# The first block's conditional layer: block-diagonal weights against two half tiles in TensorE's rows

## The chip, the cores and the metric

The kernel runs on one core of a Trainium2 chip. The core has five engines that run side by side and meet at semaphores: TensorE (PE in the profile; its weight loads are shown as PEld), VectorE (DVE), ScalarE (ACT), GpSimd (POOL) and SyncE (SP), which here only issues DMAs. The metric is the device time of one execution in microseconds; less is better. The program has 43659 instructions on the chip, and most of them belong to parts that the change leaves alone.

## The reference

The input x has 64 sequences of 64 rows (c) and 1024 columns (t). The layer that the change touches is the very first one:

```python
W = weights[condition]                     # 16 matrices of 64x64, one chosen per sequence
return jnp.einsum('bct,bcd->bdt', x, W)    # y[b, d, t] = sum over c of x[b, c, t] * W[b, c, d]
```

The full computation is an attention block on y with a residual, and then a second conditional layer (a routed low-rank addition to a dense product) with a quantized feed-forward block and a second residual:

```python
x = x + attn(cond(x, itok_B_0_15, weights), qkvw, qkvb, ow, ob)
x = x + ffn(cond2(x, itok_B_0_7, W, Wr, A, B), ...)
```

In the attention, each row d of y is a token with 1024 features t, so the products with qkvw contract over t. Everything is f32 here.

## The kernel before, in words

**Tiles and blocks.** Two sequences stacked give a tile of 128 rows (2 x 64) by 1024 columns; there are 32 tiles. Four tiles are a block (512 tokens), and there are eight blocks. The attention stage goes block by block, and within a block over four groups of heads: products for q and k, for v, then scores, softmax and context of the group before are woven in between.

**The seven-product scheme.** Products with qkvw aren't done directly. Tokens and features are split into quarters, and seven products on quarters and on sums of quarters take the place of eight (class Winograd, with the order of products in `ORDER` and their operands in `A_OF` and `B_OF`). On the side of the tokens the quarters are B11, B12, B21 and B22: the first digit is the half of the features (t below or above 512), the second the half of the block's tokens (tiles 0 and 1, or 2 and 3). The sums are T1 = B12 - B11, T2 = B22 - T1, T3 = B22 - B12 and T4 = B21 - T2, made by `t_of` (L358) on VectorE, T4 in B12's place. On the side of the weights they are S1 to S4, made by `sums` (L276, four lines L282, L283, L284 and L279) from the raw quarters A11, A21, A22 and A12.

**Product order of the first q job.** The first job (q, head group 0) takes its products in the order 1, 2, 6, 7, 5, 4, 3: A11 by B11 into bank a, A12 by B21 into the same bank, S2 by T2 into bank b, S3 by T3 into c, S1 by T1 into d, A22 by T4 into c, S4 by B22 into d. Each of these is eight records of TensorE at L509 (four f32 products, two records each). The names in the profile are psqa to psqd; the k job behind it has pska to pskd, the v job psva to psvd. Before product 2 is written into bank a, ScalarE copies the bank away (psqp, L479).

**The conditional layer of blocks 1 to 7.** `conditional_tile` (L400) lets the gathered 64x64 matrix stand in TensorE and passes x, one matrix in each half of the rows. Its result has d in the rows and t in the columns, and it is transposed by DMA. That takes long, and the work of other blocks hides it.

**The conditional layer of block 0.** There is nothing to hide it behind, so `conditional` (L367) makes a result that is transposed already: x stands, and the weights pass. `load_x` (L246) loads tile j, and POOL issues an indirect DMA (L253) that gathers the two 64x64 matrices of its two sequences into wg, 128 rows by 64 columns. VectorE fills a tile wbd with zeros (L345), and copies each wg into the two diagonal blocks of its 128x128 part (L395, two copies a tile). So one product with 128 contracted rows serves both sequences: 128 columns of x stand, the 128 columns of wbd pass, and the result has t in its rows and the tile's 128 tokens in its columns. Four such products (L380) fill one PSUM bank, which is one tile (j) and one half of t (hf). VectorE copies even tiles into the B quarter (L386), ScalarE odd ones (L388).

The order is written out by hand: the four tiles with the lower half of t, then tiles 2, 3, 0, 1 with the upper half. That way B11 and B12 are ready first, T1 is computed after the fourth product group, T2 and T3 after the sixth, and T4 after the last.

**What sets the order.** `run` (L693) takes a triple (cost, product, rest): it issues the product on TensorE, then the rest (copies and sums) of the triple before it, which waits in `behind`. The cost only advances the planner's clock `now`, from which later pieces of softmax and context get their due times. Each engine executes its own instructions strictly in the written order. PSUM tiles named "g" come from a pool of four banks, so a fifth bank waits until the first one has been copied away.

**Behind the conditional layer**, the weights' sums are issued as one list, `first_sums` (L771): four for wq on VectorE and the store of wq's S parts by a POOL DMA (L300), four for wk on POOL and their store, four for wv on POOL. POOL executes them in this order, so its store of wq, which waits for VectorE's last sum, stands ahead of the sums of wk and wv. SP's next load of a q weight goes into the buffer of the first one: it waits for that store and for the last product of the first q job.

Of the kernel before, what the change touches and what calls it, by code (L numbers as in the profile page):

```python
# [11 lines left out]
F32 = mybir.dt.float32  # L12
# [8 lines left out]
P = 128  # L21
# [15 lines left out]
def adaln_attn_ffn(ctx: ExitStack, tc: tile.TileContext, a, out: bass.AP):  # L37
# [40 lines left out]
    with tc.manual_schedule(), ExitStack() as psum, ExitStack() as early:  # L78
        ps_g = psum.enter_context(tc.tile_pool(name="ps_g", bufs=4, space=PSUM, reuse_waits="tile"))
        st = early.enter_context(tc.tile_pool(name="halve", bufs=2))  # L80
        chores = halve_weights(tc, st, const, dram, srcs, half, any_i)
        chores = itertools.chain(chores, combine_quarters(tc, st, (("wo", a["ow"]), ("wt", a["w_t"])), comb))
        op = OutProjection(tc, a, x_t, out_t, ctx_d, x1_d, ps_g, comb, KC, H)
        attention(tc, a, x_t, ctx_d, ident, dram, ps_g, KC, PB, NBLK, NCH, HPC, H, C, chores, early, op)
        second_stage(tc, a, out_t, x1_d, ident, ps_g, KC, NT, H, C, half, comb, op)
# [99 lines left out]
def attention(tc, a, x_t, ctx_d, ident, dram, ps_g, KC, PB, NBLK, NCH, HPC, H, C, chores, early, op):  # L185
# [6 lines left out]
    nc = tc.nc  # L192
    BLK = PB * P
    HB = BLK // 2
    KQ = KC // 2
# [6 lines left out]
    halves = [slice(r * C, (r + 1) * C) for r in range(2)]  # L202
# [16 lines left out]
    with ExitStack() as ctx, ExitStack() as mid:  # L219
        def pool(stack, name, bufs, **kw):  # L220
            return stack.enter_context(tc.tile_pool(name=name, bufs=bufs, reuse_waits="tile", **kw))
# [8 lines left out]
        yp = pool(mid, "y1", 1, side="right")  # L230
# [30 lines left out]
        x_of = {}  # L261
# [29 lines left out]
        def load_qk(b, wh, c, eng=None):  # L291
            t = w_qk[b, wh, c] = wp.tile([P, 7, KQ, P], F32, tag="wqk", name=f"w{wh}_{b}_{c}")
            if b == 0:
                if (wh, c) == ("q", 0):
                    held(t[:, SLOT["A11"], 0, 0:1], x_of[0, 0][1])
                for key in RAW:
                    nc.sync.dma_start(t[:, SLOT[key], :, :], quarter(key, (0 if wh == "q" else H) + c * P, P))
                return sums(
                    eng or nc.vector, lambda key: t[:, SLOT[key], :, :],
                    lambda: nc.gpsimd.dma_start(qk_d[wh, c], t[:, NR:7, :, :]),  # L300
                )
            for key in RAW:
                if SLOT[key] < NR:
                    nc.sync.dma_start(t[:, SLOT[key], :, :], quarter(key, (0 if wh == "q" else H) + c * P, P))
            nc.sync.dma_start(t[:, NR:7, :, :], qk_d[wh, c])
# [31 lines left out]
        first_sums = load_qk(0, "q", 0) + load_qk(0, "k", 0, nc.gpsimd)  # L337
# [3 lines left out]

        wbd = yp.tile([P, KC, P], F32, tag="B21", name="wbd")
        nc.vector.memset(wbd, 0.0)  # L345
        vals = [
            act.tile([P, PB, 2, 4, 2, HD], F32, tag=f"vals{g}", name=f"vals{g}") for g in range(NV)
        ]
# [2 lines left out]
        B = {}  # L351

        def quarter_of(b, key):
            return (yp if b % 2 else w).tile(
                [P, KQ, HB], F32, tag=key if b % 2 else key + "e", name=f"y{key}_{b}"
            )

        def t_of(b, Y, key, x, y):  # L358
            if key == "T4":
                Y[key] = Y["B12"]  # L360
            else:
                Y[key] = yp.tile([P, KQ, HB], F32, tag=key, name=f"{key}_{b}")
            nc.vector.tensor_tensor(Y[key], Y[x], Y[y], ALU.subtract)

        T_OF = (("T1", "B12", "B11"), ("T2", "B22", "T1"), ("T3", "B22", "B12"), ("T4", "B21", "T2"))

        def conditional():  # L367

            def one(hf, j):
                key = f"B{hf + 1}{j // 2 + 1}"  # L370
                box = []

                def product():
                    xt = x_of[0, j][0]
                    if j % 2 == 0:
                        B[key] = quarter_of(0, key)
                    ps = ps_g.tile([P, 4, P], F32, tag="g", name=f"cond_{j}_{hf}")
                    for q in range(KQ):
                        k = hf * KQ + q
                        nc.tensor.matmul(ps[:, q, :], xt[:, k * P:(k + 1) * P], wbd[:, j, :], start=True, stop=True)  # L380
                    box.append(ps)

                def rest():
                    dst = B[key][:, :, (j % 2) * P:(j % 2 + 1) * P]
                    if j % 2 == 0:
                        nc.vector.tensor_copy(dst, box[0])  # L386
                    else:
                        nc.scalar.copy(dst, box[0])  # L388
                    for n in {(0, 3): (0,), (1, 3): (1, 2), (1, 1): (3,)}.get((hf, j), ()):
                        t_of(0, B, *T_OF[n])  # L390
                return 0.95, product, rest

            for j in range(PB):
                for r in range(2):
                    nc.vector.tensor_copy(wbd[halves[r], j, halves[r]], x_of[0, j][1][halves[r], :])  # L395
            return [one(0, j) for j in range(PB)] + [one(1, j) for j in (2, 3, 0, 1)]

        Ys = [{} for _ in range(NBLK)]

# [245 lines left out]
        behind = []  # L645
# [47 lines left out]
        def run(cost, product=None, rest=None):  # L693
            nonlocal now
            while due and due[0][0] <= now + 0.01:
                heapq.heappop(due)[2]()
            if product:
                product()
            if behind:
                behind.pop()()  # L700
            if later:
                later.pop(0)()
            if rest:
                behind.append(rest)
            now += cost
# [62 lines left out]

        for f in conditional():
            run(*f)  # L770
        for f in first_sums:  # L771
            f()
        for f in qk_fill(0, 0) + v_fill(0, 0):
            run(*f)
        for b in range(NBLK):
# [3 lines left out]
            for c in range(NP):  # L779
# [15 lines left out]
                elif b + 1 < NBLK:  # L795
# [4 lines left out]
                    B = Ys[b + 1]  # L800
# [1357 lines left out]
```

## Time and profile before

| | us |
|---|---|
| median of three runs | 2379.62 (2379.28 to 2385.07) |
| the profiled execution's own time | 2369.88 |
| its span, first to last instruction | 2368.0 |
| TensorE busy in the span | 2335.0 |
| products of block 0's conditional layer (L380), first start to last end | 9.74 to 19.19 |
| first product of the q job (psqa) | 19.02 |

A group's line reads: line, engine, operation, output<-inputs, shapes, and the count behind the x; then the busy time in us, the mean of one in ns, and the idle time of the engine just before them, with what ended it. A line of the timeline or of the chain reads: start in us from the span's first instruction, length in us, engine, line, operation, tiles, count. The length runs to the end of the last one of the group. The ends of products on TensorE are modelled, and they overlap the start of the next, so the pace of a row of products is the distance of their starts.

### The profile page before, as it was taken

The page shows a single profiled execution, that of the slowest core. Times are in us where ns is not written, and L with a number is a line of the kernel's source. Part 1 is how long each engine was busy: PE and PEld are TensorE (multiplying, and loading weights), DVE is VectorE, ACT ScalarE, POOL GpSimd, SP SyncE. Part 2 cuts the span into 40 slices and gives each one's busy share as a digit, 9 for nine tenths or more (in the row PEclk, how much of TensorE's full clock was granted, in tenths as well). Part 3 has the DMA queues.
Part 4 walks back from the last instruction along what each step waited for, and adds up shares of the span by engine and source line. Part 5 has one row for each costly group of instructions (what it writes and reads, how often), then busy time and mean ns, then how long its engine had stood idle before and what let it go on. Part 6 is the DMA issues. An engine that isn't in the chain of part 4 may idle for free.

```text
span 2368.0 us, 43659 instructions
## 1 busy us (share of the span) xinstructions
PE 2335.0 (99%) x17608; PEld 1721.7 (73%) x17608; DVE 1502.4 (63%) x2887; ACT 969.4 (41%) x1333; POOL 533.9 (23%) x647
## 2 busy tenths in 40 slices
PE   8999999999999999999999999999999999999997
PEld 7888888888888888888888548888645445454553
DVE  3574474474453544643634688998577878777787
ACT  1344344344353453443433522334344454444443
POOL 4121112111122223220000357887300000000001
PEclk9999999999999999999999999999999999999999
DMA  7899799899899999997976845657944444545453
GB/s 225 201 259 243 213 215 234 227 240 214 214 243 251 231 253 251 224 229 191 184 194 187 252 164 179 218 168 238 319 80 78 83 78 83 88 75 91 75 109 86
DMA packets 612116, 437.17 MB, mean 185 GB/s; under 512 B 362433, under 2 KB 524226, under 8 KB 609986
## 3 DMA queue, kind: packets, MB, share of 16 engines
q1 hardware_dynamic: 581234, 377.13, 63.7%
q0 software_dynamic: 12240, 40.38, 7.9%
q10 hardware_dynamic: 18432, 16.79, 3.0%
q8 instruction: 141, 2.31, 0.4%
q14 instruction: 69, 0.57, 0.1%
HBM read 257.24 MB, written 91.23 MB: 147 GB/s over the span
## 4 chain that ended last, share of the span: by engine, by line
PE 94%; DMA 2%; DVE 2%; ACT 1%; issue 0%; SPq 0%; POOL 0%; ACTq 0%; DVEq 0%; POOLq 0%
PE pga L1410 6%; PE psvc L530 5%; PE psva L530 5%; PE psvd L530 5%; PE psqa L509 4%; PE pskd L509 4%; PE pskc L509 4%; PE psqd L509 4%; PE psqc L509 4%; PE pbd L1129 4%; PE pska L509 4%; PE pbc L1129 4%; PE pba L1129 4%; PE pgb L1410 3%; PE psqb L509 2%; PE pr L1711 2%
## 5 line engine op out<-in xcount | busy, mean ns | idle before, releaser
L582 ACT ACTIVATE prob<-prob 128x512 f32<-128x512 f32 x128 | 80.6, 629 | 351.0 <-DVE prob L578 351.0
L442 POOL COPY yB<-yhT 128x512 int16<-128x512 int16 (+1 forms) x84 | 76.7, 969 | 436.5 <-DMA yhT<-yh 398.5
L608 ACT COPY pT<-phT 128x1024 int16<-128x1024 int16 x128 | 165.5, 1340 | 20.5 <-DMA phT<-ph 16.0
L1949 POOL DMA_DIRECT2D out_dram<-y x29 | 25.2, 868 | 651.5 <-DVE y L1941 651.5
L596 ACT COPY ph<-prob 128x1024 int16<-128x1024 int16 x128 | 133.6, 1044 | 60.7 <-DVE prob L590 40.0
L577 DVE TENSOR_REDUCE mx<-s 128x8 f32<-128x512 f32 x128 | 87.4, 683 | 68.4 <-PE s L568 68.4
L509 PE MATMUL psqa<-yB,wq 128*128 128x256 f32 x512 | 121.1, 379 | 0.5 <-ACT psqp L479 0.5
L509 PE MATMUL pska<-yB,wk 128*128 128x256 f32 x512 | 121.0, 379 | 0.0
L530 PE MATMUL psva<-wv,yB 128*128 128x256 f32 x512 | 115.8, 379 | 0.0
L1420 ACT COPY ng<-pga 128x256 f32<-128x256 f32 x125 | 46.4, 372 | 155.8 <-PE pga L1410 138.9
L1129 PE MATMUL pba<-wtA,x1T 128*128 128x512 f32 x240 | 107.9, 592 | 0.0
L1410 PE MATMUL pga<-woS,ug_T 128*128 128x256 f32 x432 | 107.4, 380 | 0.4 <-ACT ng L1420 0.3
L530 PEld LDWEIGHTS psva<-wv,yB 128*128 128x128 f32 x512 | 97.2, 190 | 14.0 <-issue 0.8
L509 PEld LDWEIGHTS psqa<-yB,wq 128*128 128x128 f32 x512 | 97.1, 190 | 14.0 <-ACT psqp L479 0.9
L509 PEld LDWEIGHTS pska<-yB,wk 128*128 128x128 f32 x512 | 97.3, 190 | 13.2
L633 ACT ACTIVATE co<-banks,bqkv 128x256 f32<-128x256 f32 x128 | 60.7, 474 | 111.7 <-PE banks L411 81.7
L590 DVE TENSOR_TENSOR prob<-prob,den 128x512 f32<-128x512 f32 x128 | 89.2, 697 | 4.4
L578 DVE TENSOR_TENSOR prob<-s,mx 128x512 f32<-128x512 f32 x128 | 88.5, 691 | 4.5
L1410 PEld LDWEIGHTS pga<-woS,ug_T 128*128 128x128 f32 x432 | 81.8, 190 | 12.4 <-issue 0.7
L544 DVE TENSOR_TENSOR vals<-psvd,psvu 64x256 f32<-64x256 f32 (+1 forms) x96 | 40.6, 422 | 76.6 <-PE psvd L530 75.7
L588 DVE TENSOR_REDUCE den<-prob 128x8 f32<-128x512 f32 x128 | 86.4, 675 | 0.0
L1576 ACT COPY x1T<-x1h 128x1024 int16<-128x1024 int16 x64 | 81.3, 1333 | 2.7 <-DMA x1h<-x_d 2.7
(318 smaller groups left out, 5394.6 us busy)
## 6 DMA issues: line engine op xcount, KB each, us to landing
wv<-v_d SPq DMA_DIRECT2D x56, 512.0 KB, 7.7
wq<-q_d SPq DMA_DIRECT2D x28, 1024.0 KB, 8.5
wk<-k_d SPq DMA_DIRECT2D x28, 1024.0 KB, 8.7
wq<-in_qkvw_dram SPq DMA_DIRECT2D x100, 256.0 KB, 3.7
wk<-in_qkvw_dram SPq DMA_DIRECT2D x100, 256.0 KB, 5.0
wv<-in_qkvw_dram SPq DMA_DIRECT2D x50, 512.0 KB, 7.1
x<-in_x_dram SPq DMA_DIRECT2D x32, 512.0 KB, 7.4
ctx_d<-co ACTq DMA_DIRECT2D x128, 128.0 KB, 7.1
```

The costliest lines, as they stand in the source:

```text
L509: nc.tensor.matmul(ps[:, 0:HB], A[:, SLOT[A_OF[i]], k, :], B[B_OF[i]][:, k, :], start=first and k == 0, stop=k == KQ - 1, skip_group_check ...
L530: nc.tensor.matmul(ps[:, j * VC:(j + 1) * VC], B[B_OF[i]][:, k, j * P:(j + 1) * P], A[:, k, :], start=first and j == 0 and k == 0, stop=k ...
L577: nc.vector.tensor_reduce(mx, ps[:, :, n, :, :], AX.X, ALU.max)
L578: nc.vector.tensor_tensor(p.rearrange("p j h k -> p h j k"), ps[:, :, n, :, :], mx.unsqueeze(3).to_broadcast([P, HPC, 2, C]), ALU.subtract,)
L582: nc.scalar.activation(p, p, AF.Exp, scale=scale)
L588: nc.vector.tensor_reduce(den, p, AX.X, ALU.add)
L590: nc.vector.tensor_tensor(p, p, den.unsqueeze(2).to_broadcast([P, n, C]), ALU.mult)
L596: nc.scalar.copy(h, planes(p.rearrange("p n k -> p (n k)")))
L608: nc.scalar.copy(planes(pT.rearrange("p a b q -> p (a b q)")), hT)
L1129: self.nc.tensor.matmul(ps, self.B[self.B_OF[i]][:, k, :], self.A[self.A_OF[i]][:, k, :], start=first and k == 0, stop=k == self.KQ - 1, s ...
L1410: nc.tensor.matmul(s[bank], B[:, k, :], A[:, k, :], start=first and k == 0, stop=k == 1, skip_group_check=True)
L1576: nc.scalar.copy(planes(x.rearrange("p k q -> p (k q)")), s.pop(("hT", n)))
```

## The change

wbd, its memset and its copies are gone. A product now contracts 64 rows: the 64 rows of x of one sequence (halves[r]) by 128 columns stand, and that sequence's gathered 64x64 matrix passes. The two sequences of a tile use the upper and the lower half of TensorE's rows, in turn, and write to two PSUM banks: box[0] and box[1], each 128 rows (t) by 8 groups (k) of 64 tokens. A tile thus has 16 products in place of 8, and each moves 64 columns in place of 128.

The layer is worked through tile by tile, both halves of t together (cost 1.3 a tile in place of 0.95 for each of eight groups). The copies are eight on VectorE (the first sequence, L390) and eight on ScalarE (the second, L392), each of 128 by 4 by 64. The token sums T1 to T4 (now L361) have moved behind the whole layer, and they are woven with VectorE's weight sums: T1, T2, S1, S2, T3, S3, T4, S4. The rest of the last tile is issued at once, ahead of them. Lines below the change are two lower than before in part of the file and two higher at its end. The orders of instructions on POOL and SP are the same as before, and so are those on the other engines behind the first q job's start.

```diff
--- before.py
+++ after.py
@@ -341,8 +341,6 @@
 
 
 
-        wbd = yp.tile([P, KC, P], F32, tag="B21", name="wbd")
-        nc.vector.memset(wbd, 0.0)
         vals = [
             act.tile([P, PB, 2, 4, 2, HD], F32, tag=f"vals{g}", name=f"vals{g}") for g in range(NV)
         ]
@@ -366,34 +364,34 @@
 
         def conditional():
 
-            def one(hf, j):
-                key = f"B{hf + 1}{j // 2 + 1}"
+            def one(j):
                 box = []
 
                 def product():
-                    xt = x_of[0, j][0]
-                    if j % 2 == 0:
-                        B[key] = quarter_of(0, key)
-                    ps = ps_g.tile([P, 4, P], F32, tag="g", name=f"cond_{j}_{hf}")
-                    for q in range(KQ):
-                        k = hf * KQ + q
-                        nc.tensor.matmul(ps[:, q, :], xt[:, k * P:(k + 1) * P], wbd[:, j, :], start=True, stop=True)
-                    box.append(ps)
+                    xt, wg = x_of[0, j]
+                    for hf in range(2):
+                        if j % 2 == 0:
+                            B[f"B{hf + 1}{j // 2 + 1}"] = quarter_of(0, f"B{hf + 1}{j // 2 + 1}")
+                    box.extend(ps_g.tile([P, KC, C], F32, tag="g", name=f"cond_{j}_{r}") for r in range(2))
+                    for k in range(KC):
+                        for r in range(2):
+                            nc.tensor.matmul(
+                                box[r][:, k, :], xt[halves[r], k * P:(k + 1) * P], wg[halves[r], :],
+                                start=True, stop=True,
+                            )
 
                 def rest():
-                    dst = B[key][:, :, (j % 2) * P:(j % 2 + 1) * P]
-                    if j % 2 == 0:
-                        nc.vector.tensor_copy(dst, box[0])
-                    else:
-                        nc.scalar.copy(dst, box[0])
-                    for n in {(0, 3): (0,), (1, 3): (1, 2), (1, 1): (3,)}.get((hf, j), ()):
-                        t_of(0, B, *T_OF[n])
-                return 0.95, product, rest
-
-            for j in range(PB):
-                for r in range(2):
-                    nc.vector.tensor_copy(wbd[halves[r], j, halves[r]], x_of[0, j][1][halves[r], :])
-            return [one(0, j) for j in range(PB)] + [one(1, j) for j in (2, 3, 0, 1)]
+                    for hf in range(2):
+                        for r in range(2):
+                            t0 = (j % 2) * P + r * C
+                            dst = B[f"B{hf + 1}{j // 2 + 1}"][:, :, t0:t0 + C]
+                            src = box[r][:, hf * KQ:(hf + 1) * KQ, :]
+                            if r == 0:
+                                nc.vector.tensor_copy(dst, src)
+                            else:
+                                nc.scalar.copy(dst, src)
+                return 1.3, product, rest
+            return [one(j) for j in range(PB)]
 
         Ys = [{} for _ in range(NBLK)]
 
@@ -768,7 +766,11 @@
 
         for f in conditional():
             run(*f)
-        for f in first_sums:
+        behind.pop()()
+        first_tokens = [lambda n=n: t_of(0, B, *T_OF[n]) for n in range(4)]
+        for f in (
+            first_tokens[:2] + first_sums[:2] + first_tokens[2:3] + first_sums[2:3] + first_tokens[3:] + first_sums[3:]
+        ):
             f()
         for f in qk_fill(0, 0) + v_fill(0, 0):
             run(*f)
```

## The prediction

> **What bounds the kernel now.** I read the page's busy times first, then the chain of work that ended last.
>
> ```profile
> PE 2335.0 (99%) x17608; PEld 1721.7 (73%) x17608; DVE 1502.4 (63%) x2887; ACT 969.4 (41%) x1333; POOL 533.9 (23%) x647
> ...
> PE 94%; DMA 2%; DVE 2%; ACT 1%; issue 0%; SPq 0%; POOL 0%; ACTq 0%; DVEq 0%; POOLq 0%
> ```
>
> TensorE is busy in 99% of the span and carries 94% of the chain, so a change counts by what it moves on TensorE. This one touches only the first 25 us, and behind it the order of instructions is the same on every engine. So next comes the chain in order of time there (start, length, what).
>
> ```profile
> 4.46 4.62 DMA wg<-in_condw_dram,idx
> ...
> 9.17 0.31 DVE wbd L395
> ...
> 9.50 0.20 DVE wbd L395
> ...
> 9.74 9.44 PE cond L380 x64
> 19.19 1.74 PE psqa L509 x8
> ...
> 20.95 0.38 ACT psqp L479
> ...
> 21.38 1.99 PE psqa L509 x8
> 23.37 1.73 PE psqb L509 x8
> ```
>
> The first gathered block lands at 9.08, two VectorE copies put it into wbd, and TensorE starts at 9.74. The 32 products are 64 records (every f32 product is two, each with a weight load). The timeline gives the pace in two stretches, and behind them the kernel's own packed products, L568 (tiles of 32 rows by 64 columns, 64 columns passing) and L411 (64 by 64, 512 passing):
>
> ```profile
> 10.12 4.05 PE L380 MATMUL cond<-wbd,x 128*128 128x128 f32 x18
> ...
> 14.11 4.96 PE L380 MATMUL cond<-wbd,x 128*128 128x128 f32 x43
> ...
> 69.92 0.49 PE L568 MATMUL s<-kT,qT 32*64 32x64 f32 x32
> ...
> 71.45 1.99 PE L509 MATMUL psqb<-T,wq 128*128 128x256 f32 x8
> ...
> 73.28 1.89 PE L509 MATMUL psqc<-T,wq 128*128 128x256 f32 x8
> ...
> 83.88 1.09 PE L411 MATMUL banks<-x,wg 64*64 64x512 f32 x8
> ```
>
> One record there lasts 421 ns in the first stretch and 275 in the second, so starts lie (4.05-0.42)/17 = 213 ns apart, and later (4.96-0.275)/42 = 112 ns. TensorE's first 4.2 us run at about half pace, although the clock row of the page shows full speed. Last, the groups of weight loads by shape (mean ns after the bar) and VectorE's timeline behind the products:
>
> ```profile
> L509 PEld LDWEIGHTS psqa<-yB,wq 128*128 128x128 f32 x512 | 97.1, 190 | 14.0 <-ACT psqp L479 0.9
> ...
> L568 PEld LDWEIGHTS s<-kT,qT 32*64 32x64 f32 x4096 | 47.7, 130 | 11.2 <-issue 11.0
> L621 PEld LDWEIGHTS banks<-pT,vals 64*32 64x32 f32 x4096 | 42.6, 105 | 11.5 <-issue 10.7 <-ACT xh L1220 0.8
> ```
> ```profile
> 19.34 1.22 DVE L363 TENSOR_TENSOR T<-yB,yB 128x1024 f32<-128x1024 f32 x1
> ...
> 21.08 0.68 DVE L282 TENSOR_TENSOR wq<-wq 128x512 f32<-128x512 f32 x1
> ...
> 21.79 0.69 DVE L283 TENSOR_TENSOR wq<-wq 128x512 f32<-128x512 f32 x1
> ```
>
> A load's length follows its columns (105, 130, 190 ns for 32, 64, 128), not its rows: 60 ns more for 64 more columns. This is what the change must beat, since it makes 128 loads of 128 columns out of 64.
>
> **The change part by part.**
>
> *Start.* The memset of wbd (0.91 us) and its eight copies (0.20 each) go. TensorE waits for x and the gathered block itself: ScalarE's little copy that waits for the same block starts at 9.10, so I take 9.14 for 9.74: -0.60. The later blocks are copied by 11.8 at the latest, and tile 1 is wanted after 16 slow pairs, at 12.5, so no new wait.
>
> *The products.* 64 products with 64 contracted rows replace 32 with 128: 128 records, alternately in the upper and the lower half of the rows. The trace has no tile of 64 rows by 128 columns, so the price of a pair (one record in each half) is bounded. From below: if only passing columns counted, a record of 64 instead of 128 columns, 56 ns. From above: no overlap of the two halves, 2 x 112 = 224 ns. In L568, 32 records start within 0.49-0.22 = 0.27 us, 9 ns apart, though each has a load row of 130 ns, and L411's eight records of 512 columns take 1.09 us, where the full-array L1129 (107.9 us for 240) needs 0.45 each: tiles load and run together. In one half the load of 128 columns stays, and 112 ns is the pace at which such loads follow each other in L380. I take 112 ns per pair: 64 pairs, 20 of them slow, last 9.28 us as before (9.74 to 19.02). The products would end at 18.42.
>
> [...]
>
> *Leaving the packed mode.* Behind L568 the next job of eight records takes 1.99 instead of 1.89 and begins some 0.1 late: +0.2. psqa then starts at 18.62 instead of 19.02. Bounds 0 and 0.5 (around L411 TensorE stands 0.45).
>
> *Copies.* Eight copies of 128x256 on each engine (VectorE 0.42 by L482, ScalarE 0.37 by L479) replace four of 128x512 (0.69, 0.59). A tile's two take 0.84 us on VectorE, beside 1.8 us of the next tile's products; two PSUM banks per tile and four in all let tile j+2 start when tile j is copied. Only the last tile's are exposed.
>
> *VectorE's tail.* This is late next. Before, T1, T2 and T3 are computed during the products and psqb starts by TensorE's own pace at 23.21 (19.02 + 4.19). Now everything comes behind the last tile: copies from 18.6 to 19.4, T1 and T2 at 1.15 apart to 21.7, S1 and S2 at 0.7 apart to 23.1. psqb needs T2 and S2: 23.13, where TensorE would be there at 22.9. Then T3 and S3 (1.15 + 0.7) let psqc start at 24.95; before 24.94. T4 and S4 end at 26.5 and are wanted at 28. So the tail gives the 0.4 back: about 0.0.
>
> *Queues.* POOL's store of wq waits for S4, 26.6 instead of 23.8; behind it stand the sums of wk and wv, all 2.8 later. pskb (33.4) wants wk's S2, ready at 27.6 before, so 3 us of cover remain; without it pskb would wait us for us. wv's S2 moves from 36.1 to 38.9, wanted at 47. SP's next load of wq waits for that store, which lands 6.0 us after its issue: 32.8 instead of 32.0; its sums begin at 55.
>
> *Sum.* -0.60 +0.00 +0.20 +0.35 = -0.05 us. Against the profiled execution (span 2368.0, time 2369.9) that is 2369.8. The median of the runs shown is 9.7 us above that execution, so I forecast 2379.5.
>
> **Rivals.**
> - *The halves' loads do not overlap.* For: load rows grow with columns alone, and every packed product here loads at most 64. Against: L568's 9 ns. At 112 per record, 20 slow and 108 fast ones take 4.2 + 12.1 = 16.3 instead of 9.28: with the tail and the earlier start +6.9 us, 2386.5. Each ns of a pair above 112 costs about 0.06 us; it decides from a pair of some 145 ns, where the loss leaves 2 us.
> - *Load and pass follow each other in a half.* 112 plus about 56: 168 ns, some +3.4 us, 2383. Against: in L380 a load starts while the record before it still runs.
> - *The passing columns bind.* 56 ns: at half pace 39 pairs in 4.2 us and the rest in 1.4, so the products end near 14.8 and the tail starts psqb near 19.6: -3.6, 2376. The loads' length by columns speaks against it.
> - *The slow pace lasts.* If half-filled rows don't end it, 64 pairs at 213 take 13.6 and another 4.2 us pass at half pace behind: +6.0, 2385.5; with the first rival up to +20. For: nothing packed runs longer than 1.6 us in the trace. Conversely an earlier switch gains at most 20 x 0.1 = 2 us.
>
> **How the numbers follow.** Forecast 0.60, loads in series 0.13, load and pass in series 0.09, slow pace 0.07 (0.04 of it with loads in series), columns bind 0.11. The runs shown lie 5.8 us apart, so scatter adds some 2 us to each side. The range 2375 to 2388 reaches from the fastest case to the first rival and leaves the double mishap out. A difference of 0.3%, 7.1 us, is about what a measurement can tell from none: no case is that fast, so faster 0.05 is scatter; the serial loads stand at that bound and the slow pace with them over it, so slower 0.16; within 0.3% 0.79.
>
> **What would show it.** In the trace after: the first product at 9.1; 128 records in about 9.3 us, in pairs 112 ns apart behind 4.2 us at 213; psqa near 18.6; psqb waiting for VectorE's S2 and starting near 23.1; POOL's first store near 26.6 and pskb without a wait. Wrong would be a pair far from 112 ns, a slow stretch over 5 us, or a stall of pskb.

## The result: 2387.1 us, 0.5% slower than before

| | before | after |
|---|---|---|
| median, us | 2375.23 | 2387.14 |
| ratio after to before | | 1.0051, 95% interval 1.0042 to 1.0060 |
| the profiled execution's own time, us | 2369.88 | 2393.68 |
| first product of the layer, us | 9.74 | 8.79 |
| first product of the q job (psqa), us | 19.02 | 22.64 |
| psqb, us | 23.21 | 29.01 |

The forecast was a difference of -0.05; it is about +12 (0.0051 x 2375 = 12.1, interval 10 to 14). The profiled execution after is 6.5 above its own median and the one before 5.4 below, so between the two profiles lie 23.8.

**The head** (all up to psqb). The page after has TensorE as the bound again, with some idle time more (the lines that answer to the first ones of before):

```profile
PE 2348.8 (98%) x17672; PEld 1731.7 (72%) x17672; DVE 1499.5 (63%) x2882; ACT 970.8 (41%) x1337; POOL 534.0 (22%) x647
...
PE 90%; DVE 2%; DMA 2%; SPq 1%; issue 1%; ACT 1%; POOL 0%; ACTq 0%; DVEq 0%; POOLq 0%
```

The timeline of TensorE after shows the layer in one piece, and the q job behind it (start, length, then as before):

```profile
8.79 13.92 PE L378 MATMUL cond<-wg,x 64*128 64x64 f32 x128 [8.79 <-DMA wg<-in_condw_dram,idx]
22.64 3.78 PE L507 MATMUL psqa<-yB,wq 128*128 128x256 f32 x8
26.88 2.29 PE L507 MATMUL psqa<-yB,wq 128*128 128x256 f32 x8 [0.46 <-ACT psqp L477]
29.01 1.89 PE L507 MATMUL psqb<-T,wq 128*128 128x256 f32 x8
```

128 records in 13.92 us are 64 pairs, (13.92-0.42)/63 = 214 ns apart: each at the slow pace, to the last. And the first eight records of psqa take 3.78, where the same eight took 1.89 before:

```profile
19.02 1.89 PE L509 MATMUL psqa<-yB,wq 128*128 128x256 f32 x8
```

Each record's own length (the answer for line L378: min/median/max in ns, first and last start) says the same:

```profile
L378 PEld LDWEIGHTS cond<-wg,x x128: 285/330/335, 8.8 to 22.2; 64*128 64x128 f32 x128
L378 PE MATMUL cond<-wg,x x128: 417/417/473, 8.8 to 22.3; 64*128 64x64 f32 x128
```

417 ns is what a record of before lasted in its first 4 us (421), and a load of 330 stands beside 190 for loads of 128 columns at full clock. So TensorE ran at half clock for 18.7 us (8.79 to 27.51) where before it did so for 4.3 (9.74 to 14.05). The ends of these stretches are the first entries of the granted clock in the two traces, both of 1.00; ahead of its first entry a trace has none, the windows print 1.00, and the pace alone tells the clock: the first records of psqa start 427 ns apart, as those of psqb do where the trace after has an entry of 0.50 (from 164.04 on), and those of psqb at 29.01 start 216 apart. That costs 5.8 at psqb. VectorE is not what psqb waits for: T2 and S2, predicted as late next, are ready at 27.3.

**Behind the head.** psqb is 5.8 late, and up to 155 us the two traces keep that distance. Then it grows in steps. Windows of the trace after (busy time and records of each engine, then the granted clock, the DMA share and GB/s) have two stretches below full clock:

```profile
155.00:190.00 35.00, 29.27 (x239) 24.36 (x238) 20.17 (x38) 10.45 (x15) 5.29 (x6) 0.90 1.15 238
...
380.00:410.00 30.00, 26.82 (x234) 21.88 (x234) 6.38 (x12) 13.67 (x17) 4.86 (x6) 0.89 1.04 249
```

In the same stretches of before it is 1.00:

```profile
155.00:190.00 35.00, 33.94 (x331) 29.14 (x322) 27.10 (x47) 14.26 (x19) 4.56 (x6) 1.00 1.02 229
...
380.00:410.00 30.00, 30.00 (x264) 25.78 (x257) 12.78 (x25) 12.27 (x18) 6.00 (x8) 1.00 0.98 253
```

TensorE's timeline after shows what stands ahead of each slow piece:

```profile
159.80 1.46 PE L566 MATMUL s<-kT,qT 32*64 32x64 f32 x112
164.21 0.52 PE L566 MATMUL s<-kT,qT 32*64 32x64 f32 x16 [2.96 <-issue]
164.67 3.36 PE L507 MATMUL psqb<-T,wq 128*128 128x256 f32 x8
...
183.12 2.45 PE L507 MATMUL pskc<-T,wk 128*128 128x256 f32 x8 [2.55 <-DVE qT L492]
```

TensorE stops for 2.96 in the middle of a row of 128 scores, and it is not another engine's work that ends the wait ("issue"). Then the granted clock is 0.50 for 3.4 us (psqb 3.36 instead of 1.89). At 400 the same happens in psvc, with 3.18. Of the 23.8 between the profiles, 5.8 are the head, 11.0 more idle time between 30 and 2330 us (17.4 against 6.4), and 6.8 the half of 13.6 us at half clock in three pieces (3.4 and 6.8 at the two stalls, and 3.4 from 184.5 on, behind the 2.55 that pskc waits for VectorE's qT).

So there are two questions: why does the clock stay down in the packed products, and is the loss far behind the layer the change's, or chance?

### The profile page after: what moved, and what is told of

Read it like the earlier page. It is cut to its first block, busy times and chain, and to the rows that moved or that the text cites. A ratio compares the mean times of both kernels' runs of the same rounds, so it can differ in the third digit from the quotient of the medians.

```text
span 2391.9 us, 43791 instructions
## 1 busy us (share of the span) xinstructions
PE 2348.8 (98%) x17672; PEld 1731.7 (72%) x17672; DVE 1499.5 (63%) x2882; ACT 970.8 (41%) x1337; POOL 534.0 (22%) x647
## 3 DMA queue, kind: packets, MB, share of 16 engines
q8 instruction: 141, 2.31, 0.4%
## 4 chain that ended last, share of the span: by engine, by line
PE 90%; DVE 2%; DMA 2%; SPq 1%; issue 1%; ACT 1%; POOL 0%; ACTq 0%; DVEq 0%; POOLq 0%
PE pga L1412 5%; PE psvc L528 4%; PE psvd L528 4%; PE pskd L507 4%; PE pskc L507 4%; PE psva L528 4%; PE pbc L1131 4%; PE pbd L1131 4%; PE pba L1131 4%; PE pska L507 4%; PE psqa L507 4%; PE psqd L507 4%; PE psqc L507 4%; PE pgb L1412 3%; PE pr L1713 2%; PE pskb L507 2%
```

## The experiments

Four theories. *Duty*: the clock stays down because TensorE passes only 64 columns for each load of 128. *Rows*: because only half of the rows, or two halves in turn, are used. *Blocks*: TensorE's instructions are fetched in blocks of 256 (the page's queue "q8 instruction" has 141 packets and 2.31 MB, 16 KB each; TensorE has 35344 records and 422 semaphore and other instructions, so 254 a packet; that the queue is TensorE's, and 256 to a block, is an estimate from these numbers, for the places of the stalls to bear out); the change adds 64 matmul records with a load each, 128 in all, so every block behind it ends at other work, and some of these ends stall. *Chance*: stalls come anywhere, in any kernel.

In the table, the loss is (ratio - 1) times the median of before in the same comparison; "behind the head" is the loss less what psqb is later in the trace than the mean of two traces of before (22.9). The shift is what the kernel adds to TensorE's count of instructions ahead of the scores (up to 2 semaphore instructions more are left out). By its interval alone each number of the last column is open by 2 to 5 either way, and psqb comes from one trace each; the two of before differ by 0.65.

| kernel | median (before) | ratio, 95% | psqb | shift | behind the head |
|---|---|---|---|---|---|
| before, again | 2371.03 (2371.95) | 0.9992 (0.9981-1.0004) | 22.56 | 0 | -1.6 |
| before, 64 tiny products | 2373.53 (2369.12) | 1.0011 (1.0001-1.0021) | 23.65 | 256 | 1.8 |
| changed, 32 tiny | 2381.54 (2372.18) | 1.0036 (1.0020-1.0051) | 28.68 | 256 | 2.7 |
| the same, again | 2380.45 (2369.12) | 1.0043 (1.0029-1.0058) | 28.40 | 256 | 4.7 |
| changed, warm-up | 2375.26 (2371.95) | 1.0013 (1.0002-1.0024) | 22.07 | 256 | 3.9 |
| changed, wide, warm-up | 2371.44 (2371.95) | 1.0002 (0.9990-1.0013) | 22.80 | 256 | 0.6 |
| changed | 2387.14 (2375.23) | 1.0051 (1.0042-1.0060) | 29.01 | 128 | 6.0 |
| changed, again | 2380.07 (2369.12) | 1.0048 (1.0033-1.0064) | 28.16 | 128 | 6.1 |
| changed, 64 tiny | 2386.71 (2369.12) | 1.0066 (1.0050-1.0082) | 29.83 | 384 | 8.7 |
| before, 32 tiny | 2376.82 (2372.18) | 1.0023 (1.0011-1.0036) | 22.05 | 128 | 6.3 |
| before, warm-up | 2376.74 (2371.95) | 1.0020 (1.0008-1.0032) | 21.26 | 128 | 6.4 |
| changed, wide | 2376.12 (2372.18) | 1.0011 (0.9998-1.0023) | 23.16 | 128 | 2.3 |
| before, narrow | 2395.42 (2372.18) | 1.0093 (1.0071-1.0114) | 42.43 | 128 | 2.5 |

### What keeps the clock down: wider and narrower passes

*The changed kernel, 128 columns pass.* A bank then holds four groups, so each tile goes one half of t after the other.

```diff
+        wide = w.tile([P, PB, 2 * C], F32, tag="wide", name="wide")
+        nc.vector.memset(wide, 0.0)
...
-            wg = xp.tile([P, C], F32, tag="wg", name=f"wg_{i}", bufs=4)
+            if b == 0:
+                wg = wide[:, j, :]
+            else:
+                wg = xp.tile([P, C], F32, tag="wg", name=f"wg_{i}", bufs=4)
...
-                out=wg[:, :],
+                out=wg[:, 0:C],
...
-            def one(j):
+            def one(j, hf):
...
-                    box.extend(ps_g.tile([P, KC, C], F32, tag="g", name=f"cond_{j}_{r}") for r in range(2))
+                    box.extend(ps_g.tile([P, KQ, 2 * C], F32, tag="g", name=f"cond_{j}_{hf}_{r}") for r in range(2))
...
-                        src = box[r][:, hf * KQ:(hf + 1) * KQ, :]
+                        src = box[r][:, :, 0:C]
```

> The changed kernel with 128 instead of 64 columns passing in each product of a half: the gathered block lies in the left half of a tile of zeros, the products of the right half are not used, and the outputs are the same. The products stay 128, in pairs, one in each half of TensorE's rows. Theory of the duty: TensorE stays at half clock because it passes only 64 columns for each load of 128; with 128 columns it reaches full clock some 4 to 5 us after its start, pairs go at about 112 behind that, 20 slow pairs and 44 fast ones take 9.2, and psqb begins at about 23. Rival, the half-filled rows or the two halves at once keep the clock down: all 64 pairs at 213, psqb at about 29 as in the changed kernel. Second rival, two halves with twice the columns don't go side by side: 64 pairs at 213 or more even at full clock, psqb past 29. Time: 2381 by the duty, 2387 by the rivals, if the rest of the loss stays.

*The kernel before, 64 columns pass, full rows.*

```diff
-                        nc.tensor.matmul(ps[:, q, :], xt[:, k * P:(k + 1) * P], wbd[:, j, :], start=True, stop=True)
+                        for r in range(2):
+                            nc.tensor.matmul(
+                                ps[:, q, halves[r]], xt[:, k * P:(k + 1) * P], wbd[:, j, halves[r]],
+                                start=True, stop=True,
+                            )
```

> The kernel before, with each product on full rows split in two of 64 passing columns: the same 128 rows of weights loaded twice, outputs the same, 128 products instead of 64. Theory of the duty: 64 columns for each load of 128 keep the clock at half, so all 128 products go at 213, 27.3 in sum: psqa begins near 37 and psqb past 41, 18 more than before. Rival, half-filled rows were the reason: full rows release the clock after some 4.3 us, 20 products at 213 and 108 at 112 make 16.4, psqa begins near 26, psqb near 30, about 7 more than before.

TensorE's timeline in the wide kernel, and then in the narrow one:

```profile
8.77 10.02 PE L383 MATMUL cond<-wide,x 64*128 64x128 f32 x128 [8.77 <-DMA wide<-in_condw_dram,idx]
18.72 1.99 PE L511 MATMUL psqa<-yB,wq 128*128 128x256 f32 x8
...
23.16 1.97 PE L511 MATMUL psqb<-T,wq 128*128 128x256 f32 x8
```
```profile
9.05 27.57 PE L381 MATMUL cond<-wbd,x 128*128 128x64 f32 x128 [9.05 <-DVE wbd L399]
36.41 3.73 PE L513 MATMUL psqa<-yB,wq 128*128 128x256 f32 x8
40.60 1.99 PE L513 MATMUL psqa<-yB,wq 128*128 128x256 f32 x8 [0.46 <-ACT psqp L483]
42.43 1.89 PE L513 MATMUL psqb<-T,wq 128*128 128x256 f32 x8
```

With the same loads, the same rows and twice the columns to pass, the layer is 3.90 shorter (10.02 against 13.92); the clock is full from 14.3 on and psqb is where it was before. With full rows and half the columns, all 128 products go at 213 ns for 27.5 us and psqa still begins at half pace (full clock from 40.5 on). Both are the numbers of the duty theory (psqb 23 and past 41), and the rows are ruled out. That the two halves work side by side is shown on the way: 80 records in the wide kernel between 14.02 and 18.79 are 40 pairs, about 115 ns each.

### Does TensorE keep the full clock through narrow passes: a warm-up

The 32 products stand ahead of the layer, in the time in which TensorE waits for the gather, and they write a tile that nobody reads. They run somewhat past that time: until 10.1 in the changed kernel, 9.6 in the kernel before and 11.1 in the wide one.

```diff
+        pad = ps_s.tile([P, 4, 512], F32, tag="s", name="pad")
+        for _ in range(6):
+            nc.tensor.matmul(pad[0:32, 0, 0:16], ident[0:32, 0:32], ident[0:32, 0:16], start=True, stop=True)
+        for _ in range(26):
+            nc.tensor.matmul(pad[:, 1, 0:P], ident, ident, start=True, stop=True)
```

On the changed kernel:

> The changed kernel with the same 32 products ahead of the conditional layer. Question: does TensorE, once at full clock, keep it through packed products of 64 columns. If it does, 64 pairs at about 107 take 6.9, psqa begins near 16 and psqb near 21, where VectorE's last sums (5 behind the last product) begin to set it. [...] Whole time against before: -2 + 4 = +2 in the first case, +5 to +9 in the second.

On the kernel before:

> The kernel before, with 26 full products of the identity by itself (128 columns) and 6 tiny ones ahead of the conditional layer, in the time in which TensorE waits for the gather. Theory of the duty: TensorE is at full clock when the layer starts at about 9.2 to 9.7, its 64 products take 107 each, 6.9 in sum, psqa begins near 16.5 instead of 19.0 and psqb near 20.8 instead of 23.2. If only time since the start counts and not work, psqb stays at 23.2. Whole time: the head's 2.4 less, and 4 to 6 more if any change to TensorE's list of instructions costs that: +2 to +4; or -2.4 if the padding cost nothing.

On the changed kernel with 128 columns passing:

> The changed kernel with 128 columns passing (zeros in the right half) and the same 32 products ahead: both ways to the full clock together. Pairs at about 107 from 8.8 on, 64 of them take 6.9, psqa near 16, psqb between 20.3 by TensorE and 21 by VectorE's last sums, 2.2 to 2.9 ahead of before. Whole time: -2.5 if nothing else costs; +1.5 to +3.5 if a change to TensorE's list of instructions costs 4 to 6.

The changed kernel with the warm-up: the answer for its products, and the timeline behind.

```profile
L383 PEld LDWEIGHTS cond<-wg,x x128: 183/188/188, 10.1 to 17.1; 64*128 64x128 f32 x128
L383 PE MATMUL cond<-wg,x x128: 272/272/320, 10.1 to 17.2; 64*128 64x64 f32 x128
```
```profile
10.08 7.36 PE L383 MATMUL cond<-wg,x 64*128 64x64 f32 x128
17.37 1.99 PE L512 MATMUL psqa<-yB,wq 128*128 128x256 f32 x8
19.83 1.99 PE L512 MATMUL psqa<-yB,wq 128*128 128x256 f32 x8 [0.46 <-ACT psqp L482]
22.07 1.99 PE L512 MATMUL psqb<-T,wq 128*128 128x256 f32 x8 [0.25 <-DVE wq L288]
```

The clock came up at 6.2, and the same packed products of 64 columns keep it for 7.4 us: no load is longer than 188 ns, and 64 pairs take 7.36. So for these 7.4 us narrow passes did not take away the clock that was there; in the changed kernel they failed for 13.92 us to bring it up. A loss of it came with long waits: in the trace after, those of 2.96, 2.55 and 3.18 stand at the pieces with a granted clock of 0.50, 3.41, 3.41 and 6.83 us long. Why the narrow passes leave the clock as it was, down in one trace and up in the other, is not shown.

The prices of the prediction come out of the same lines: with the clock up, a pair starts 112 ns behind the one before, and psqb waits 0.25 for VectorE's S2 and starts 4.63 behind the layer's end (22.07 - 17.44); the prediction had 4.71. The warm-up on the kernel before brings psqb to 21.26, 1.6 ahead of the mean of before; in the wide kernel the clock came up only at 8.2 and the warm-up itself ran until 11, so its psqb is 22.80. None of the three beats before: 1.0013, 1.0020 and 1.0002, the last with an interval that holds 1 (0.5 us slower; expected were 2.5 faster by the head alone, or 1.5 to 3.5 slower).

### Where the rest goes: moving the ends of the blocks

*The kernel before and the changed kernel, 32 tiny products ahead of the layer.*

```diff
+        pad = ps_s.tile([P, 4, 512], F32, tag="s", name="pad")
+        for _ in range(32):
+            nc.tensor.matmul(pad[0:32, 0, 0:16], ident[0:32, 0:32], ident[0:32, 0:16], start=True, stop=True)
```

The tile that they write is read by nobody. In the trace of the kernel before with them they are 64 matmul records and 64 weight loads, from 1.39 to 4.99: 128 records, as many as the change adds.

> The kernel before, with 32 tiny products (32 columns of the identity as weights, 16 columns pass, full precision) put ahead of the conditional layer, while TensorE has nothing else to do. [...] Theory of instruction fetch: the blocks in which TensorE's instructions are fetched end at other places, as they do in the changed kernel, so stalls of 2 to 3 us and a slowed clock behind them appear in the scores or the contexts; the head is as before (psqb from about 23.2), and the median goes up by about 6, to about 2381. Rival, all of the loss comes from the head or its shift in time: the median stays within 2 of before's, 2373 to 2377.

> The changed kernel with the same 32 tiny products ahead of the conditional layer, so that its count of TensorE instructions differs from before's by twice what the change added. Theory of instruction fetch in blocks: the two shifts together are one whole block, the blocks end again where they ended before, the two long stalls (161.3 and about 397) go away, and only the head's 5.8 is left: about 2381, 6 less than the changed kernel. Rival, the stalls follow from the shift of the work in time by 5.8 us, or come by chance: the stalls stay and the time is the changed kernel's, about 2387.

*The kernel before, unaltered.*

> The kernel before, unaltered, timed against itself. The four variants so far lost between 3.9 and 5.8 more than their heads explain: the padded kernel before gained 1.2 at its head and lost 4.6 in its median. If that is how the comparison leans, this run shows a loss of 3 to 6 too. If any change to TensorE's list of instructions costs it, this run shows none: a ratio of 1.000, within 0.0013, and the losses belong to the variants.

The padded kernel before loses 0.23% though its psqb is 0.8 early, so the loss behind the head needs no packed products. The comparison does not lean: before against itself is 0.9992. The changed kernel with 32 tiny products has a loss between those of the two theories. Its trace had two stalls of "issue" (1.5 and 1.3), at other places. Four more kernels take this further:

*The changed kernel, unaltered; with 64 tiny products; the kernel before with 64; the changed kernel with 32, again* (the edit is that above, with 32 or 64).

> The changed kernel, unaltered, for a second trace and a second comparison. Head: psqb from about 29, 5.8 to 6.4 behind before. In the traces so far every stall of TensorE of 0.3 and more that nothing but the fetch of its own instructions ends lies at one residue (193 or 194) of its count of instructions modulo 256. Theory: the change has moved its list by 128, and so the ends of the blocks of 256 now lie at other work; here the stalls appear at counts 2497, 3009, 7362 or 10433, one or more of them, and the whole loses 10 to 14. Rival, chance: stalls at counts of other residues, or none, and a loss of 6 to 8.

> The changed kernel with 64 tiny products ahead of the layer: 256 instructions more, so that the ends of the blocks lie where they lie in the changed kernel. By the blocks: the loss behind the head, which is the whole loss less what the trace shows at psqb, stays at about 5 (4 to 7), with stalls at counts 256 further on (2753, 3265, 7618, 10689). By a rival, in which any added work costs alike or stalls come by chance: the loss behind the head is that of the changed kernel with 32 tiny products, about 2 to 3. The tiny products run until about 8.2 and may bring the clock up early; then psqb starts before 24, as with the warm-up, and the head's 5.8 is gone.

> The kernel before with the 64 tiny products: 256 instructions more, so the ends of the blocks lie at the same work as in before. By the blocks: no loss behind the head, where the same kernel with 32 tiny products lost about 6; the whole time is before's or up to 2.4 less, if the tiny products bring the clock up before the layer starts (ratio 0.998 to 1.001). By the rival that any added product at the start costs: 3 to 6 slower.

> The changed kernel with 32 tiny products once more, beside the changed kernel itself on one chip. By the blocks: psqb at about 29 in both, and this one is faster by 3 to 5 (a loss of 6 to 9 against before, where the changed kernel's is 10 to 14). By chance: the two lose the same within 2.

**The places.** All stalls of "issue" of 0.3 us and more between 30 and 2330 us, with their place in TensorE's count of records (matmuls, weight loads and semaphore instructions) from the start, worked out from the traces:

```
shift 0:         none (two traces)
shift 256:       64 tiny: none          32 tiny: 14529 (1.5), 27074 (1.3)    again: none
                 warm-up: 20161 (0.4)   wide, warm-up: none
shift 128, 384:  changed: 2497 (3.0), 7362 (3.2), 14160 (0.4)   again: 7362 (1.9)   narrow: 7361 (1.4), 10433 (0.5)
                 before, 32 tiny: 3009 (0.5)    before, warm-up: 3009 (1.1), 7362 (0.6)    wide: 10433 (1.0)
                 changed, 64 tiny: 10690 (0.4), 13761 (0.6)
```

Except for one (14160), each is 193 or 194 above a multiple of 256: 2497 = 9 x 256 + 193, 7362 = 28 x 256 + 194. The same place is hit in different kernels, as two lines of each show. Before with 32 tiny products and before with the warm-up stop after the same 126 of 128 scores:

```profile
181.39 1.58 PE L571 MATMUL s<-kT,qT 32*64 32x64 f32 x126
183.47 0.27 PE L571 MATMUL s<-kT,qT 32*64 32x64 f32 x2 [0.50 <-issue]
```
```profile
178.80 1.58 PE L573 MATMUL s<-kT,qT 32*64 32x64 f32 x126
181.45 0.27 PE L573 MATMUL s<-kT,qT 32*64 32x64 f32 x2 [1.08 <-issue]
```

and the changed kernel (second trace) and the narrow one after the same 11 of 16 records of psvc:

```profile
387.41 2.64 PE L528 MATMUL psvc<-wv,T 128*128 128x256 f32 x11
391.95 1.35 PE L528 MATMUL psvc<-wv,T 128*128 128x256 f32 x5 [1.90 <-issue]
```
```profile
400.74 2.64 PE L534 MATMUL psvc<-wv,T 128*128 128x256 f32 x11
404.83 1.24 PE L534 MATMUL psvc<-wv,T 128*128 128x256 f32 x5 [1.45 <-issue]
```

That these stalls stand at one place of a count modulo 256 is shown, and the packets of q8 tie them to the fetch: in 13 of the 14 the last packet ahead landed 1.3 to 1.6 us before the stall's end (2.5 in the other, at 14529), and had started only 0.5 to 2.4 us before TensorE stopped. So these stalls were the longer the later the packet started and the longer it took. The one at 164 had its packet from 160.74 to 162.65, half a microsecond ahead of its beginning; ahead of the one at 400 the packet took 3.67, where most take about 1.0. Why a packet starts late is not shown. Each of the seven traces with an odd multiple of 128 has a stall, and two of seven of the others. Most packets come with none: the trace after has two such stalls for its 141 packets.

**A second cost of the same shift.** With the count shifted by 128 or 384, a packet of q8 starts 4.0 to 6.9 us behind the start of the DMA transposes of yh (at 144 to 164 us) in six of seven traces, and 9.3 behind it in the first trace after; otherwise it comes 8.6 to 11.3 behind. The transposes then last 6.2 to 12.7 (mean 7.9 of seven), otherwise 4.0 to 6.9 (mean 5.4 of seven). Behind them on SP stands the load of wk, which VectorE waits for, ahead of qT. The changed kernel (second trace) and then the changed kernel with 32 tiny products (second run), on SP, VectorE and TensorE:

```profile
150.16 7.62 SPq L426 DMA_TRANSPOSE yhT<-yh  x2
...
161.44 4.93 SPq L297 DMA_DIRECT2D wk<-in_qkvw_dram  x4
```
```profile
171.36 0.69 DVE L282 TENSOR_TENSOR wk<-wk 128x512 f32<-128x512 f32 x1 [3.48 <-DMA wk<-in_qkvw_dram]
```
```profile
177.43 1.99 PE L507 MATMUL pskc<-T,wk 128*128 128x256 f32 x8 [2.55 <-DVE qT L492]
```
```profile
152.02 4.83 SPq L429 DMA_TRANSPOSE yhT<-yh  x2
...
159.82 4.75 SPq L300 DMA_DIRECT2D wk<-in_qkvw_dram  x4
```
```profile
168.77 0.69 DVE L285 TENSOR_TENSOR wk<-wk 128x512 f32<-128x512 f32 x1 [0.41 <-DMA wk<-in_qkvw_dram]
```
```profile
174.99 1.89 PE L510 MATMUL pskc<-T,wk 128*128 128x256 f32 x8
```

pskc waits 2.1 to 2.6 in six of the seven traces with the ends moved (0.2 in the seventh, before with the warm-up), and 0 to 1.0 in the others. That such a packet and slow transposes come together is shown; that the one makes the other slow was not tried by itself.

**The times.** Behind the head, the seven kernels with the ends moved lose 2.3 to 8.7, on average 5.5; the other six lose -1.6 to 4.7, on average 2.0 (2.7 without the unaltered kernel before). The two groups overlap: the wide and the narrow kernel lose 2.3 and 2.5, where about 6 had been expected of the wide one. Idle time of TensorE between 30 and 2330 us is 10 to 17 in the traces of the former, 6 to 13 in those of the latter. The traces add up: from psqb to the end, less this idle time and half of the time at half clock, each of the fourteen takes 2336 to 2340. The two terms together are 15.8 on average in the seven traces with the ends moved and 9.1 in the other seven. Of the difference of 6.7 (5.3 without the first trace after), the stalls of "issue" are 1.6, the half clock 2.2 and the wait of pskc 1.9.

The prediction on the changed kernel with 64 tiny products (4 to 7 behind the head, stalls 256 further on) came out as 8.7, above it, with a stall at 10690 as named and one at 13761. The changed kernel again lost 11.4 in all (10 to 14 had been expected), with one stall, at 7362, one of the places named. The kernel before with 64 tiny products lost 1.8, and not nothing, where with 32 it lost 6.3. The direct comparison failed: the changed kernel with 32 tiny products was to be 3 to 5 faster than the changed kernel beside it, and the medians were 2380.45 and 2380.07. By its ratio it is 1.2 faster, far inside the uncertainty of either (about 3.5). Between the kernels of the two groups as a whole the difference is 3.5; one pair could not show it. The tiny products did not bring the clock up early: psqb did not move ahead of 28 in any changed kernel that had only these.

## Why the prediction was wrong

- *Start, 9.14.* Right in kind: TensorE waits for the gathered block itself. It started at 8.79, since the block landed some 0.35 earlier in that run; the second trace has 8.64.
- *The products, "64 pairs, 20 of them slow".* **This is the step that failed.** The price of a pair was right: 112 ns at full clock, measured with the warm-up, so the halves do load and pass side by side. The loads of the two halves do not add up: in series, at the 112 ns between L380's records, 128 would take 14.3, and they took 7.36. What failed is the number of slow pairs, taken over from the kernel before: 64 in place of 20, 13.9 us in place of 9.28. I had taken the slow first 4.2 us as a time that passes, which was an estimate from that one stretch; in these runs the slow pace ended only where 128 or more columns passed per load (14.05 before, 14.3 in the wide kernel), and with 64 it lasted to the end of the layer and beyond (27.51).
- *The rival "the slow pace lasts"* had the place and the price: +6.0 at psqb, of which 4.2 in the pairs and the rest in a psqa at half pace; the trace has 5.8. Its condition named the wrong feature. Half-filled rows did not keep the clock down (wide kernel, full from 14.3 on); half-filled passes did, on full rows too (narrow kernel, from 40.5 on).
- *The prices put down for the warm-up.* No run shows the 107 of those expectations (half of the 216 ns between L509's records of 256 columns is 108): the pairs of the changed kernel start 112 apart, those of the wide one about 113, the products of the kernel before 112 to 116 (8 in 1.06, 56 in 6.63). Nor does a run show the +5 to +9 for a clock that is lost again in the layer: it stayed up, and the changed kernel with the warm-up lost 3.1.
- *Leaving the packed mode, +0.20.* With the clock up, psqa starts 0.1 later than one more pair would, and takes 1.99 instead of 1.89: right.
- *Copies, 0.84 a tile.* Two took 0.76.
- *VectorE's tail.* Right where it can be seen: with the clock up psqb waits for S2, 4.63 behind the layer against 4.71 predicted. In the changed kernel the slow psqa hides it.
- *Queues.* POOL's store of wq came at 31.06 instead of 26.6, 4.5 later with the layer, and pskb had no wait there: the cover was enough.
- *"Behind it the order of instructions is the same on every engine", hence nothing there.* This is the second thing that was missing, about half of the loss: 6.0 of 12.1. The order is the same, its place in the count modulo 256 is not. Shifts by 128 alone cost the kernel before 6.3 and 6.4 behind the head. Where the shift is 256, the five altered kernels still lose 2.7 on average. What that is stays open: in the best trace of such a kernel (the changed one with 32 tiny products, second run) no stall of 0.3 by "issue" is left.

The forecast of 2379.5 differs from 2387.1 by 7.6: the head's 5.8 and the 6 behind it, less 4.4 by which the medians of before differ in the two sets of runs. That it still lies in the range of 2375 to 2388 is in good part luck: half of the loss comes from a place that was put at nothing, and with the median of before that the forecast went by, the time would be near 2391.7 (2379.62 + 12.1).

## What to carry to other kernels

Ahead of splitting products into narrower ones at the start of a program, count the columns that pass for each column that is loaded: at 64 for 128 TensorE did not leave half clock here (13.9 us, and 27.5 on full rows), and the price of a tile at full clock was the wrong one. Passing zeros to fill 128 columns brought the clock up at 14.3, and full products ahead of the first real one at 6.2. And 128 more TensorE records at the start of this unrolled program moved every later one in the count modulo 256 at which 14 of the 15 stalls stand; in this kernel (DMA share about 1.0 in the windows above) that was worth 3.5 us between the averages of the two groups and 6.3 on the kernel before, as much as the half clock at the start, so a difference of 0.2% needs a padded control before it is put down to the edit.

## What the runs showed of the hardware that was not expected

- 64 columns passing for each load of 128 columns kept TensorE at half clock on full rows (128 products, 27.5 us, 213 ns apart) and on two half-filled groups of rows (64 pairs, 13.9 us); 128 columns passing on the same half rows brought it up after 5.5.
- Once up, the clock stayed through 7.4 us of the same 64-column products.
- Twice as many columns passed cost next to nothing: at full clock the wide kernel's pairs go at about 115 ns, those of 64 columns at 112.
- Stalls of TensorE with no other engine in them stood 193 or 194 above a multiple of 256 in its count of records in 14 of 15 cases, 0.4 to 3.2 us long, and ended 1.3 to 1.6 us (once 2.5) behind the landing of a packet of the queue q8; at two of them, of 3.0 and 3.2 us, the granted clock was 0.50 for 3.4 and 6.8 us.
